# Diagonal key tiles moved from the end of each attention unit to behind its first two full tiles

## The chip, the cores and the metric

The kernel runs on one core of one Trainium2 chip. The metric is the device time of one execution in microseconds (us); the time before is the median of three executions. Five engines of the core matter here: PE (the matrix engine), DVE (the vector engine), ACT (the scalar engine), POOL and SP; the last two mostly issue transfers. Matrix products are written to PSUM, which DVE and ACT then read.

## The reference

A sequence of 2048 tokens of width 256 passes through four residual blocks: attention a, FFN, attention b, FFN. Each block adds its result to x, and each reads a layer-normalised x. Cut to what matters:

```python
# attention (16 heads of 16; a: 4 key/value heads and rotary angles and biases; b: 16 key/value heads)
scores = einsum('bthd,bshd->bhts', q, k) * head_dim ** -0.5
scores = where(tril(ones((S, S))), scores, -inf)      # a query sees itself and earlier keys
out = softmax(scores) @ v ; x = x + out @ Wo.T
# FFN: Wg, Wu, Wd are unpacked from 4-bit codes and scales
x = x + (gelu(xn @ Wg.T) * (xn @ Wu.T)) @ Wd.T
```

The softmax is over all earlier keys, so a query block needs the largest score of each row before its exponentials, and the order in which key tiles are summed is free.

## The kernel before

**Units.** Queries are cut into four blocks b of 512 (`TB`). Sixteen heads are four groups g of four. A *unit* is one (b, g); each attention layer runs its 16 units in order, b outermost. `Attention.run` writes the instruction order of all engines by hand.

**The value pass of a unit** (`value_steps`) goes over key tiles kt of 128 keys: 4b full ones, and four *diagonal* ones, in which the mask cuts a triangle and the queries before the tile are left out: N = 512, 384, 256 and 128 queries. Each key tile takes two *steps* p = 0, 1, each for two of the four heads:

- `pair(kt, p)`: takes a PSUM tile `ps_s`, subtracts the row maxima by a small product (L758, operand `mT`), and adds the scores (L763). For a full tile ACT's exponential (L775, tile `e`) is issued at once. For a diagonal one it is *owed*: four mask products (L645) and the exponential follow when the next `settle()` is called, which is in the next `pair`, in `values`, or ahead of the next maximum if a masked maximum is owed too.
- `values(half)`: sums e times v of the key tile before into the one PSUM tile `ps_av` (L743), 256 queries at a time. Of the third and fourth diagonal tile (256 and 128 queries) all is summed in half 0 and half 1 is empty.

The sums of the last key tile are done by `end()`, with a copy of `ps_av` to `o` on ACT (L790); `divide()` turns `o` (L797) and divides. Both are put into the next unit's steps 0 and 2.

**The maxima of the next unit** (`max_steps`) are computed beside it: for query tile i and key block c the scores again, queries on the partitions (L670), into `ps_s`, and a DVE reduction (L682). For c < b the tile has 512 keys; for c = b, the diagonal, (i + 1) * 128 keys and mask products. The last step, `gather`, joins the partial maxima in five short DVE instructions (L694 to L704) and leaves them in `m_pad`; `turn` transposes `m_pad` on PE (L711, four products), and ACT copies the result to `mT` (L717). The next unit's first `pair` reads `mT`.

**What sets the order.** `ps_s` has three buffers, taken in turn by pairs and maxima: the fourth taker waits until the first one's exponential or reduction is done. `weave(main, side, rest=3)` puts the maxima and other side work (`more`: projections of the next block, the output projection, unpacking of FFN weights) between a step's `pair` and its `values`; three of a unit's maxima go to steps 0 to 2 (four where the next unit is longer by half or a third, six in the step from b = 0 to b = 1), the others are spread over the rest but the last three steps. So the last three steps of a unit have no side work, and `gather` is in the fourth from the end. `turn` stands at the start of the last step, before its `pair`. PE, DVE and ACT each run their instructions in the order written. A unit of block b has 8(b + 1) steps, and as many maxima as its next unit has steps.

**Order of tiles before.** Value pass: full tiles, then the diagonal ones (N = 512, 384, 256, 128). Maxima: full ones, then the diagonal ones with 128, 256, 384 and 512 keys.

Of the kernel before, what the change touches and what calls it, by code (L numbers as in the profile page):

```python
# [31 lines left out]
NT = TB // P  # L32
# [47 lines left out]
def tile_hybrid_layers(  # L80
# [40 lines left out]
    def ps_s():  # L121
        return psum.tile([P, 2, 512], F32, tag="s", name="ps_s", bufs=3)
# [4 lines left out]
    def ps_m():  # L127
        return psum.tile([P, 512], F32, tag="m", name="ps_m")
# [278 lines left out]
    class Attention:  # L407
# [251 lines left out]
        def max_steps(self, b, g):  # L659

            held = {}

            def scores(i, c, p):
                if not held:
                    held["mx"] = self.wk.tile([P, NT, 4, NB], F32, tag="mx", name="mx")
                w = TB if c < b else (i + 1) * P
                self.settle("max")
                pt = ps_s()
                for r in range(2):
                    nc.tensor.matmul(  # L670
                        pt[:, r, :w],
                        lhsT=self.qT[b, g][64 * r : 64 * r + 64, p, i * P : (i + 1) * P],
                        rhs=self.key_rows(c, g, p, r, slice(0, w)),
                        start=True, stop=(c < b),
                    )

                def masked():
                    self.add_mask(pt, 0, w - P)
                    reduced()

                def reduced():
                    nc.vector.tensor_reduce(  # L682
                        held["mx"][:, i, 2 * p : 2 * p + 2, c], pt[:, :, :w], AX.X, ALU.max
                    )

                if c == b:
                    self.owed.append(("max", masked))
                else:
                    reduced()

            def gather():
                self.settle()
                nm = self.wk.tile([P, NT, 4], F32, tag="nm", name="nm")
                nc.vector.tensor_reduce(  # L694
                    nm, held["mx"][:, :, :, : b + 1], AX.X, ALU.max, negate=True
                )

                to = m_pad[:, :, :, :6].rearrange("q t r (p s) -> q t p r s", s=3)
                rest = nm.rearrange("q t (p r) -> q t p r", r=2)
                nc.vector.tensor_copy(to[:, :, :, :, 0], rest)  # L700
                less = self.wk.tile([P, NT, 2, 2], F32, tag="rest", name="rest")
                nc.vector.tensor_tensor(less, rest, to[:, :, :, :, 0], ALU.subtract)
                nc.vector.tensor_copy(to[:, :, :, :, 1], less)
                nc.vector.tensor_tensor(  # L704
                    to[:, :, :, :, 2], less, to[:, :, :, :, 1], ALU.subtract
                )

            def turn():
                pt = ps_m()
                for i in range(NT):  # L710
                    nc.tensor.matmul(  # L711
                        pt[:, i * P : (i + 1) * P],
                        lhsT=m_pad[:, i].rearrange("p r c -> p (r c)"), rhs=ident_b,
                        start=True, stop=True,
                    )
                self.mT[b, g] = self.wk.tile([P, TB], BF16, tag="mT", name="mT")
                nc.scalar.copy(self.mT[b, g], pt)  # L717


            tiles = [(i, c) for c in range(b + 1) for i in range(NT)]  # L720
            steps = [lambda i=i, c=c, p=p: scores(i, c, p) for i, c in tiles for p in range(2)]
            return steps + [gather], turn

        def value_steps(self, b, g):

            nk = NT * (b + 1)
            held = {"pending": []}

            def values(half):

                self.settle()
                kt, q0, es_ = held["pending"][0]
                few = TB - q0 <= TB // 2
                if half == 1:
                    held["pending"].pop(0)
                    if few:
                        return
                elif kt == 0:
                    held["av"] = ps_av()
                own = slice(q0, TB) if few else slice(*((q0, TB // 2), (TB // 2, TB))[half])  # L740
                for j in range(4):
                    h = g if self.first else 4 * g + j
                    nc.tensor.matmul(  # L743
                        held["av"][32 * j : 32 * j + 32, own],
                        lhsT=self.vv[kt // NT][:, kt % NT, h * VW : h * VW + 32],
                        rhs=es_[j // 2][:, j % 2, own],
                        start=(kt == 0 and half == 0), stop=(kt == nk - 1),
                    )

            def pair(kt, p):  # L750
                q0 = max(0, kt - NT * b) * P
                diagonal = kt >= NT * b
                keys = slice((kt % NT) * P, (kt % NT + 1) * P)
                self.settle()
                pt = ps_s()

                for r in range(2):
                    nc.tensor.matmul(  # L758
                        pt[:, r, q0:], lhsT=sel[64 * r : 64 * r + 64, p, :],
                        rhs=self.mT[b, g][64 * r : 64 * r + 64, q0:], start=True, stop=False,  # L760
                    )
                for r in range(2):
                    nc.tensor.matmul(  # L763
                        pt[:, r, q0:], lhsT=self.key_rows(kt // NT, g, p, r, keys),
                        rhs=self.qT[b, g][64 * r : 64 * r + 64, p, q0:],
                        start=False, stop=not diagonal,
                    )
                e = self.wk.tile([P, 2, TB], F32, tag="e", name="e", bufs=4)

                def masked():  # L770
                    self.add_mask(pt, 1, q0)
                    exponentials()

                def exponentials():
                    nc.scalar.activation(e[:, :, q0:], pt[:, :, q0:], AF.Exp, scale=QK_SCALE)  # L775

                if diagonal:
                    self.owed.append(("exp", masked))
                else:
                    exponentials()  # L780
                if p == 0:
                    held["es"] = [e]
                else:
                    held["pending"].append((kt, q0, held["es"] + [e]))

            def end():
                values(0)
                values(1)
                o = pre.tile([P, TB], F32, tag="o", name="o")
                nc.scalar.copy(o, held["av"])  # L790
                held["o"] = o

            def divide():
                o = held["o"]
                pt = ps_m()
                for i in range(NT):
                    nc.tensor.transpose(  # L797
                        pt[:, i * P : (i + 1) * P], o[:, i * P : (i + 1) * P], ident
                    )
                heads = pt.rearrange("p (t j c) -> p t j c", t=NT, c=32)  # L800
                rec = small.tile([P, NT, 4], F32, tag="rec", name="rec")
                nc.vector.reciprocal(rec, heads[:, :, :, HD])
                if g == 0:
                    self.att[b] = pre.tile([P, NT, NG, 4, HD], F32, tag="att", name="att")
                nc.vector.tensor_tensor(
                    self.att[b][:, :, g], heads[:, :, :, :HD],
                    rec.unsqueeze(3).broadcast_to([P, NT, 4, HD]), ALU.mult,
                )

            steps = []  # L810
            for kt in range(nk):
                for p in range(2):
                    scored = lambda kt=kt, p=p: pair(kt, p)
                    steps.append((scored, lambda p=p: values(p)) if kt else scored)
            return steps, end, divide

        def out_steps(self, b):
# [30 lines left out]
        def run(self, extra, beside):  # L848
# [5 lines left out]
            for n, (b, g) in enumerate(units):  # L854
# [3 lines left out]
                if g == 0 and b + 1 < NB:  # L858
                    ahead = self.prep_steps(b + 1)

                    few = -(-(len(ahead) - (7 if self.first else 5)) // 2)
# [7 lines left out]
                maxima, turn = [], None  # L869
                if n + 1 < len(units):  # L870
                    maxima, turn = self.max_steps(*units[n + 1])
                else:
                    more += beside
                steps, end, divide = self.value_steps(b, g)
# [2 lines left out]
                    scored, *summed = steps[at] if isinstance(steps[at], tuple) else (steps[at],)  # L877
                    steps[at] = (scored, step, *summed)
                if turn:
                    scored, summed = steps[-1]  # L880
                    steps[-1] = (turn, scored, summed)
                first = len(maxima) * 3 // len(steps)
                weave(steps[:3], maxima[:first])
                weave(steps[3:], blend(maxima[first:], more) if maxima else more, rest=3)
# [96 lines left out]
    with tc.tile_pool(name="wk1", bufs=2) as wk, tc.tile_pool(name="kv1", bufs=1) as kv:  # L981
        at.wk = at.qpool = wk
        with tc.tile_pool(name="init", bufs=1) as pool:
# [13 lines left out]
            steps, turn = at.max_steps(0, 0)  # L997
# [6 lines left out]
    with tc.tile_pool(name="kv20", bufs=1, reuse_waits="tile") as kv0, tc.tile_pool(  # L1004
# [8 lines left out]
        steps, turn = at.max_steps(0, 0)  # L1013
# [60 lines left out]
```

## Time and profile before

| | us |
|---|---|
| median of 3 executions (lowest to highest) | 1888.08 (1885.3 to 1889.78) |
| the profiled execution, and its span | 1890.76, span 1888.9 |
| PE busy | 1766.7 (94%) |
| DVE busy | 1123.3 (59%) |
| ACT busy | 805.2 (43%) |
| POOL busy | 239.0 (13%) |
| reductions of the maxima, L682 (640) | 658.2 |
| exponentials, L775 (640) | 571.3 |

Stretches of single units, from the first L758 of a unit to that of the next, with the busy time of each engine in it:

| unit (layer, b, g) | stretch, us | length | PE | DVE | ACT |
|---|---|---|---|---|---|
| b, 3, 1 | 1409.45:1455.86 | 46.41 | 45.11 | 36.70 | 30.96 |
| b, 2, 3 (the next one has b = 3) | 1318.48:1358.26 | 39.78 | 36.34 | 35.48 | 22.97 |
| b, 1, 3 (the next one has b = 2) | 1164.22:1193.92 | 29.70 | 25.07 | 26.03 | 14.79 |
| b, 1, 1 | 1104.75:1134.70 | 29.95 | 28.30 | 19.32 | 16.03 |
| b, 0, 2 | 1035.11:1053.13 | 18.02 | 16.72 | 8.60 | 8.05 |

How to read the profile: a group's line gives the kernel line, engine, operation, tiles written and read, count, busy time, mean duration, and the idle time before it with what ended most of it. A wait line gives the waiting instruction, the one waited for, the total, how often, and the longest. A timeline line gives start, duration, engine, line, tiles and count, with the idle time before it in brackets. PE's products are pipelined, so successive ends, not durations, tell how long each took.

### The profile page before, as it was taken

Reading aid. Unit: us, or ns where it says so; the run is one execution under the profiler, and the core shown is the slowest. Engines: PE = TensorE matmul, PEld = TensorE weight load, DVE = VectorE, ACT = ScalarE, POOL = GpSimd, SP = SyncE. Lnnn points to the kernel's source line nnn. Section 1 sums busy time; section 2 is a strip of 40 time slices with the busy share of each in tenths; the row PEclk is TensorE's granted clock in tenths of the full one; section 3 lists DMA queues with packets and bytes.
Section 4 is the critical chain, followed back from the end, with each engine's and each line's share of the span. In section 5 each row is a group of like instructions: output and inputs, shape, how many; then the busy total and the mean of one; then the engine's idle time right before and its main releaser. Section 6 shows DMA issues by size and latency. Waiting matters only on the chain. (4 is left out here: it accounts for less than half of the span.)

```text
span 1888.9 us, 31839 instructions
## 1 busy us (share of the span) xinstructions
PE 1766.7 (94%) x13452; PEld 928.5 (49%) x13452; DVE 1123.3 (59%) x1676; ACT 805.2 (43%) x1069; POOL 239.0 (13%) x437
## 2 busy tenths in 40 slices
PE   5788889999999999999998898999999999999999
PEld 3344444444444456656564444444444444756656
DVE  4567687778786253544445667766877715363442
ACT  1334455555667531222213355556566662131221
POOL 4111321210001011112101010010000001011110
PEclk8889999999999999999998999999999999999999
DMA  4421310310101100001303232041000010000000
GB/s 100 108 60 37 68 52 23 63 35 24 35 24 35 45 6 1 1 0 42 81 1 74 62 72 54 12 90 33 15 13 2 2 46 1 11 1 11 7 6 12
DMA packets 42271, 64.24 MB, mean 34 GB/s; under 512 B 13840, under 2 KB 20880, under 8 KB 41872
## 3 DMA queue, kind: packets, MB, share of 16 engines
q1 hardware_dynamic: 33488, 45.93, 8.2%
q0 software_dynamic: 7680, 15.74, 5.0%
q8 instruction: 106, 1.74, 0.4%
q10 hardware_dynamic: 960, 0.52, 0.1%
q14 instruction: 37, 0.30, 0.1%
HBM read 44.24 MB, written 17.83 MB: 33 GB/s over the span
## 5 line engine op out<-in xcount | busy, mean ns | idle before, releaser
L682 DVE TENSOR_REDUCE mx<-ps_s 128x2 f32<-128x1024 f32 (+3 forms) x640 | 658.2, 1060 | 221.0 <-PE ps_s L645 116.0
L775 ACT ACTIVATE e<-ps_s 128x1024 f32<-128x1024 f32 (+3 forms) x640 | 571.3, 897 | 422.6 <-PE ps_s L763 244.8
L743 PE MATMUL ps_av<-e,v 128*32 128x256 f32 (+1 forms) x4608 | 365.2, 384 | 3.4 <-ACT e L775 3.4
L763 PE MATMUL ps_s<-qT,kT 64*128 64x512 f32 (+3 forms) x1280 | 341.7, 527 | 0.0
L670 PE MATMUL ps_s<-kT,qT 64*128 64x512 f32 (+3 forms) x1280 | 269.2, 423 | 52.3 <-DVE mx L682 22.8
L758 PE MATMUL ps_s<-mT,sel 64*128 64x512 bf16 (+3 forms) x1280 | 232.7, 358 | 27.3 <-ACT mT L717 10.1
L934 PE MATMUL ps_s<-xnT,wg 128*128 128x512 f32 x512 | 242.1, 595 | 0.0
L934 PE MATMUL ps_s<-xnT,wu 128*128 128x512 f32 x512 | 240.6, 592 | 0.0
L670 PEld LDWEIGHTS ps_s<-kT,qT 64*128 64x128 f32 x1280 | 130.1, 188 | 161.6 <-ACT e L775 66.5
L758 PEld LDWEIGHTS <-sel 64*128 64x128 bf16 x1280 | 75.0, 93 | 251.2 <-issue 242.3
L942 DVE TENSOR_TENSOR t<-ps_s,t 128x512 f32<-128x512 f32 x128 | 88.1, 688 | 164.5 <-POOL t L941 162.7
L940 ACT ACTIVATE t<-ps_s 128x512 f32<-128x512 f32 x128 | 76.2, 595 | 251.8 <-PE ps_s L934 251.3
L943 ACT ACTIVATE t<-t 128x512 f32<-128x512 f32 x128 | 80.6, 629 | 200.7 <-DVE t L942 200.7
L934 PEld LDWEIGHTS ps_s<-xnT,wu 128*128 128x128 f32 x512 | 97.3, 190 | 122.7 <-issue 122.7
L941 POOL TENSOR_SCALAR t<-t 128x512 f32<-128x512 f32 x128 | 79.1, 618 | 573.0 <-ACT t L940 572.5
L743 PEld LDWEIGHTS ps_av<-e,v 128*32 128x32 f32 x4608 | 95.0, 108 | 109.1 <-issue 89.5
L934 PEld LDWEIGHTS ps_s<-xnT,wg 128*128 128x128 f32 x512 | 96.0, 192 | 106.0 <-issue 104.0
L944 DVE SCALAR_TENSOR_TENSOR t<-t,ps_s 128x512 f32<-128x512 f32 x128 | 88.0, 688 | 89.0 <-ACT t L943 89.0
L763 PEld LDWEIGHTS ps_s<-qT,kT 64*128 64x128 f32 x1280 | 130.5, 199 | 0.0
L959 PE MATMUL ps_m<-wd,inter 128*128 128x256 f32 x512 | 114.5, 380 | 0.0
L959 PE MATMUL ps_av<-wd,inter 128*128 128x256 f32 x512 | 114.5, 380 | 0.0
L959 PEld LDWEIGHTS ps_av<-wd,inter 128*128 128x128 f32 x512 | 96.7, 190 | 17.1 <-issue 4.5
(125 smaller groups left out, 1179.9 us busy)
## 6 DMA issues: line engine op xcount, KB each, us to landing
qT<-h SPq DMA_DIRECT2D x256, 64.0 KB, 2.2
kT<-h POOLq DMA_DIRECT2D x96, 128.0 KB, 5.9
h<-high SPq DMA_DIRECT2D x24, 256.0 KB, 2.6
h<-low SPq DMA_DIRECT2D x24, 256.0 KB, 2.5
wd<-wd_kept SPq DMA_DIRECT2D x2, 2048.0 KB, 7.8
wd_kept<-dq_d SPq DMA_DIRECT2D x4, 512.0 KB, 2.7
out<-x SPq DMA_DIRECT2D x16, 128.0 KB, 1.7
x<-x SPq DMA_DIRECT2D x3, 512.0 KB, 5.4
```

The costliest lines, as they stand in the source:

```text
L670: nc.tensor.matmul(pt[:, r, :w], lhsT=self.qT[b, g][64 * r : 64 * r + 64, p, i * P : (i + 1) * P], rhs=self.key_rows(c, g, p, r, slice(0, w)),
L682: nc.vector.tensor_reduce(held["mx"][:, i, 2 * p : 2 * p + 2, c], pt[:, :, :w], AX.X, ALU.max)
L743: nc.tensor.matmul(held["av"][32 * j : 32 * j + 32, own], lhsT=self.vv[kt // NT][:, kt % NT, h * VW : h * VW + 32], rhs=es_[j // 2][:, j % ...
L758: nc.tensor.matmul(pt[:, r, q0:], lhsT=sel[64 * r : 64 * r + 64, p, :], rhs=self.mT[b, g][64 * r : 64 * r + 64, q0:], start=True, stop=False,)
L763: nc.tensor.matmul(pt[:, r, q0:], lhsT=self.key_rows(kt // NT, g, p, r, keys), rhs=self.qT[b, g][64 * r : 64 * r + 64, p, q0:], start=Fals ...
L775: nc.scalar.activation(e[:, :, q0:], pt[:, :, q0:], AF.Exp, scale=QK_SCALE)
L934: nc.tensor.matmul(pt[:, k, :], lhsT=w[:, c, fc * P : (fc + 1) * P], rhs=self.xnT[b][:, c, :], start=(c == 0), stop=(c == 1),)
L941: nc.gpsimd.tensor_scalar(t, t, GELU_A, 1.0, ALU.mult, ALU.add)
L942: nc.vector.tensor_tensor(t, gate, t, ALU.mult)
L943: nc.scalar.activation(t, t, AF.Tanh, scale=GELU_C)
L944: nc.vector.scalar_tensor_tensor(t, t, 1.0, gate, ALU.add, ALU.mult)
L959: nc.tensor.matmul(po[:, :D], lhsT=inter[:, fc, i * P : (i + 1) * P], rhs=wd[:, fc, :], start=(fc == 0), stop=(fc == NFC - 1),)
```

## The change

In a unit with full tiles the value pass now takes the first two full key tiles, then the four diagonal ones, then the other full ones. The maxima take the first two full tiles, then the diagonal ones in falling size (512, 384, 256, 128 keys), then the other full ones. For b = 0 there are no full tiles: the value pass is as before, and the maxima run in reverse. The start and stop marks of the accumulation follow the first and last tile of the new order. `turn` moves from the start of the last step to the middle of the last but one: behind its `pair`, ahead of its `values`. The number and kind of instructions is the same.

```diff
-            tiles = [(i, c) for c in range(b + 1) for i in range(NT)]
+            full = [(i, c) for c in range(b) for i in range(NT)]
+            tiles = full[:2] + [(i, b) for i in reversed(range(NT))] + full[2:]
...
-            nk = NT * (b + 1)
+            full = [*range(NT * b)]
+            order = full[:2] + [*range(NT * b, NT * (b + 1))] + full[2:]
...
-                elif kt == 0:
+                elif kt == order[0]:
                     held["av"] = ps_av()
...
-                        start=(kt == 0 and half == 0), stop=(kt == nk - 1),
+                        start=(kt == order[0] and half == 0),
+                        stop=(kt == order[-1] and (few or half == 1)),
...
-            for kt in range(nk):
+            for kt in order:
                 for p in range(2):
                     scored = lambda kt=kt, p=p: pair(kt, p)
-                    steps.append((scored, lambda p=p: values(p)) if kt else scored)
+                    first = kt == order[0]
+                    steps.append(scored if first else (scored, lambda p=p: values(p)))
...
                 if turn:
-                    scored, summed = steps[-1]
-                    steps[-1] = (turn, scored, summed)
+                    scored, summed = steps[-2]
+                    steps[-2] = (scored, turn, summed)
```

## The prediction

> **What bounds the kernel now.** First the page: PE is busy for 1766.7 of 1888.9 us, and the largest group elsewhere is DVE's reductions.
>
> ```profile
> span 1888.9 us, 31839 instructions
> PE 1766.7 (94%) x13452; PEld 928.5 (49%) x13452; DVE 1123.3 (59%) x1676; ACT 805.2 (43%) x1069; POOL 239.0 (13%) x437
> L682 DVE TENSOR_REDUCE mx<-ps_s 128x2 f32<-128x1024 f32 (+3 forms) x640 | 658.2, 1060 | 221.0 <-PE ps_s L645 116.0
> ```
>
> The waits say what PE's attention work waits for: PSUM tiles held by ACT or DVE, and `mT` and `m_pad` between units.
>
> ```profile
> PEld ps_s L670 <- ACT e L775: 66.5, 176, 1.6
> PEld ps_s L670 <- DVE mx L682: 60.0, 128, 1.6
> PE ps_s L758 <- ACT mT L717: 10.1, 29, 0.7
> PE ps_m L711 <- DVE m_pad L704: 8.3, 7, 3.5
> ```
>
> Then the timeline: a plain full step, the middle of the diagonal ones, and the seam between two units (all from layer b, b = 3).
>
> ```profile
> 1422.05 0.40 PE L743 MATMUL ps_av<-e,v 128*32 128x256 f32 x4
> 1422.42 0.58 PE L763 MATMUL ps_s<-qT,kT 64*128 64x512 f32 x2
> 1422.83 0.48 PE L670 MATMUL ps_s<-kT,qT 64*128 64x512 f32 x2
> 1423.24 0.64 PE L743 MATMUL ps_av<-e,v 128*32 128x256 f32 x8
> ...
> 1448.72 0.29 PE L645 MATMUL ps_s<-mask_t,mask_w 64*128 64x64 bf16 x8
> 1449.05 1.02 ACT L775 ACTIVATE e<-ps_s 128x1024 f32<-128x1024 f32 x1 [0.67 <-PE ps_s L645]
> 1449.55 0.47 PE L763 MATMUL ps_s<-qT,kT 64*128 64x384 f32 x2
> 1450.13 0.50 PE L670 MATMUL ps_s<-kT,qT 64*128 64x512 f32 x2
> ...
> 1454.55 0.23 DVE L704 TENSOR_TENSOR m_pad<-rest,m_pad 128x16 bf16<-128x16 f32 x1
> 1455.46 0.40 PE L711 MATMUL ps_m<-ident_b,m_pad 128*128 128x128 bf16 x4
> 1455.90 0.58 ACT L717 CAST mT<-ps_m 128x512 bf16<-128x512 f32 x1 [0.45 <-PE ps_m L711]
> 1456.54 0.39 PE L758 MATMUL ps_s<-mT,sel 64*128 64x512 bf16 x2 [0.32 <-ACT mT L717]
> 1457.45 0.43 PE L743 MATMUL ps_av<-e,v 128*32 128x128 f32 x8
> 1459.73 0.51 PE L670 MATMUL ps_s<-kT,qT 64*128 64x512 f32 x2 [0.27 <-ACT e L775]
> ```
>
> I count PE by differences of ends. The sums end at 1422.45, the pair at 1423.00, the maximum at 1423.31, the next sums at 1423.88: pair 0.55, maximum 0.31 (0.24 where no buffer was awaited), sums 0.57, a step 1.36 to 1.44. In the same way a pair with N = 384, 256, 128 takes 0.44, 0.34, 0.28, sums of 128 queries 0.36, masks 0.07 each. In a queue the reductions take 1.14 each, as the chain shows where DVE binds (the unit b, 1, 3):
>
> ```profile
> 1170.75 12.54 DVE mx L682 x11
> ```
>
> At 1.15 maxima a step that is 1.31 us of DVE, just below PE's step. So PE leads by little, and a lighter PE step makes DVE or ACT the bound.
>
> **The change part by part.** No instruction is added or removed; no DMA moves, so SP and POOL keep their order. All cost is in waits. I write a "full-seam unit" for one whose predecessor has b of 1 or more (22 of 32).
>
> *Seam, gain 0.64.* Before, the first pair of a unit ends 0.95 after its predecessor rather than 0.55 (the 0.32 wait for `mT`). Then ACT holds the buffers: the second maximum takes 0.46 for 0.24, the third 0.85 for 0.24 (at 1459.73 it waits for an exponential queued behind the copy `o`); with 0.05 at the first, 1.28. After the change `turn` (0.33) is followed by sums 0.57, a pair 0.55 and sums 0.57, 1.69 us, while ACT needs about 1.02 for the exponential ahead and 0.58 for `mT`, begun with `turn`: the 0.40 goes. `end` has two full sums, 1.14 for 0.36, which hides all but the third maximum's wait: the exponential before it starts behind `o` and ends some 1.1 after its pair, PE is there after 0.24 + 0.55, 0.64 stays. 1.28 - 0.64 = 0.64.
>
> *Diagonal steps, loss 0.86.* The rule read at 1450.13: masks end at 1449.01, the exponential runs 1449.05 to 1450.07, and the next but one maximum, which needs its buffer, ends 0.61 after its pair rather than 0.25: a wait of 0.36. Before, such terms in the unit b, 3, 1 are 0.27 (a pair behind two small maxima), 0.10, 0.22, 0.36, 0.15: 1.10. After, both passes shrink together and the maxima wait behind exponentials of 1.02, 1.02, 0.81, 0.81 and 0.60 us with pairs of 0.55, 0.44, 0.44, 0.34 and 0.34 for cover: 0.20, 0.32, 0.10, 0.21, 0.23, then 0.06. The half-1 steps without sums, which before lay in the tail without maxima, now lie among full maxima: over four steps PE has about 4.0 us (1.28, 0.66, 1.24, 0.85), DVE 4 x 1.23 less overlaps; PE waits 0.14 + 0.07 + 0.14 for reductions and 0.22 + 0.27 for full exponentials, 0.84. Sum 1.96, less 1.10. The trace has no diagonal pair beside a shrinking diagonal maximum: the bounds are 0 (side work covers as before) and 1.7 (nothing overlaps). I take 0.86, from the neighbouring rows' own durations.
>
> *Turn behind the pair of the last step but one.* Waiting there, it holds sums, the last step and the next unit's first pair. From the last maximum to `turn` PE has, for b of 2 and 3, sums 0.57, pair 0.55, sums 0.57, pair 0.55, sums 0.57, pair 0.55 = 3.36; DVE needs 0.1 + 1.23 + 1.2 for the five gather instructions = 2.55. No wait. For b = 1 two of the sums are empty and one short, 2.0 at the end against 2.55, or 3.7 with two maxima queued: 0.5 to 1.6, less what projections (1.9 each) cover. I take 0.5 against 0.15 before: loss 0.35.
>
> By the Trainium skill (TensorE: Matmul & The Clock Gate, Part 3, The mechanism) matmuls are strict FIFO, "no reordering", though weight loads may pass; the timeline agrees, for nothing of PE passes a waiting L711. Could PE go round it, the 0.35 above and the turn's share of the next class would be zero and the forecast about 4 us lower.
>
> *Units by class.* Block 3 and 2, not g = 3 (12): 0.86 - 0.64 = +0.22 each, +2.6. Block 1, not g = 3 (6): +0.22 + 0.35, +3.4; two of them follow b = 0 and gain only 0.40 at the seam, +0.5. Block 1 into 2 (2): DVE binds; its chain (work 25.9 in a queue, idle 1.0 at the start, 1.7 to 1.85 within) ends as late as before, and behind it come `turn`, sums, pair, sums = 2.1 rather than 1.1: +1.15 each, +2.3. Block 2 into 3 (2): same tail, but diagonal maxima no longer end a stretch that DVE binds: +0.2 each, +0.4. Block 0 into 1 (2): DVE's chain as long, tail +0.25: +0.5. Last unit of each layer: 0.40 and 0.29 (divide behind `o`) gone, 0.4 for the last full exponential: -0.3 each, -0.6. Block 0 (6): the reverse order lets the small reductions end last, so turn waits of 1.68, 0.79 and 0.24 and buffer waits of some 5 us near the end shrink, while full maxima in the first steps cost about 0.95 each: -2.8, the least certain. The first maxima of layer a, alone on PE: the first reduction starts later, +0.3. FFN stages: nothing moves.
>
> Sum: 2.6 + 3.4 + 0.5 + 2.3 + 0.4 + 0.5 - 0.6 - 2.8 + 0.3 = +6.6 us. The profiled execution's 1890.76 (span 1888.9 and 1.86 around it) becomes 1897.4. It lies 2.7 above the median of the runs; on the median 1888.08 the forecast is 1894.7, 0.35% slower. About 0.2% (3.8 us) is what a measurement of this kernel can tell from no change.
>
> The skill also says (Perfetto Trace Analysis, Optimization Strategy) that stages with different bounds may gain by interleaving. That speaks for moving small maxima among the full ones, and the classes with b rising agree only in part: what DVE regains in the middle it loses in a longer tail. If interleaving won there, the 2.3 + 0.4 would be about -2 and the sum 2.
>
> **Rivals.** *Faster, by the seam.* The place: diagonal steps whose waits stay at 1.10 because projections and unpacking stand between. Then 18 units gain 0.86 each, 15.5, and the block-1 turns do not wait, 2.1: 6.6 - 17.6 = -11, 1877. For it: blocks 0 to 2 have much side work. Against: blocks 3 have little, and most of what there is runs on DVE. It decides where a unit's diagonal waits stay below about 1.96 - 6.6 / 18 = 1.6.
>
> *No change.* Turn waits in block 1 covered by projections and DVE stretches no worse: 6.6 - 2.1 - 2.3 = +2.2, 1890.3. For it: one of three block-1 units in layer b waits at `turn` now. Against: the two sums that covered are gone.
>
> *Much slower, DVE becomes the bound.* A reduction is 1.14 in a queue at 1.15 to 1.22 a step, so a backlog after the light steps melts by under 0.1 a step; at 0.8 or more of it `turn` waits in blocks 2 and 3 too, some 0.6 in 12 units, +7.2: 1902. For it: unpacking puts more on DVE in layer a (38.6 against 36.7 us a unit). Against: three buffers let PE run only that far ahead.
>
> **How the numbers follow.** Main case 0.44, much slower 0.18, no change 0.22, faster 0.16. Slower by over 0.2%: 0.44 + 0.18 = 0.62; within: 0.22; faster: 0.16. The range leaves out half the faster case and the far end of the slower: 1883 to 1905. The cases from the main one's own bounds reach 1890 to 1901.
>
> **What would show it.** Right: no wait of L758 for `mT` in units after b = 1 or more; more waits of L670 and L758 for L775 and L682 in steps 5 to 14 of a unit; L711 waiting for `m_pad` in block-1 units for 0.5 us; unit b, 3, 1 near 46.6, unit b, 1, 3 near 30.8. Wrong: b = 3 units shorter than 46.2, or reductions queued without a gap in them.

## The result and the profile after

Five executions of the changed kernel have a median of 1899.58 us (1897.06 to 1900.07), five of the kernel before 1889.78 (1885.3 to 1890.63): a ratio of 1.0054, 95% interval 1.0039 to 1.0068. The profiled execution took 1900.07 us, 9.3 more than that of before. The forecast was +0.35%, in a range that holds the time. But the total hides errors that cancelled: where I expected most of the loss there was none, and the seams between blocks cost far more, in part for a reason that the forecast doesn't have.

The page of the changed kernel: span, engines and the reductions. (From L720 on, line numbers are 1 to 5 higher than before: L758, L763, L743, L775 are now L762, L767, L746, L779.)

```profile
span 1898.3 us, 31835 instructions
PE 1774.0 (93%) x13452; PEld 921.8 (49%) x13452; DVE 1119.1 (59%) x1676; ACT 808.2 (43%) x1069; POOL 238.8 (13%) x437
L682 DVE TENSOR_REDUCE mx<-ps_s 128x2 f32<-128x1024 f32 (+3 forms) x640 | 657.2, 1061 | 234.7 <-PE ps_s L670 124.7
```

The same 13452 products keep PE busy 7.3 us longer, and its idle time grew by only 2.1: most of the loss is products whose records are longer. Of the waits, the one of L758 (now L762) for `mT` fell from 10.1 us (29 times) to 1.3 (the first units of the two layers), and the one of the maxima for DVE grew from 22.8 to 27.7. The first line is the trace before, the others the trace after:

```profile
PE ps_s L670 <- DVE mx L682: 22.8, 47, 1.2
```

```profile
PEld ps_s L670 <- ACT e L779: 74.5, 177, 1.2
PEld ps_s L670 <- DVE mx L682: 58.4, 109, 1.6
PE ps_s L670 <- DVE mx L682: 27.7, 57, 1.2
PE ps_m L711 <- DVE m_pad L704: 8.3, 8, 2.0
PE ps_s L762 <- ACT mT L717: 1.3, 2, 0.7
```

**Where it went.** Unit lengths of the two traces, from the first L758 (L762) of a unit to that of the next, summed by the classes of the prediction (the stretches ahead of the prediction start and end up to 0.7 us before that product; their lengths are the same):

| class (units) | forecast, us | trace after less trace before, us |
|---|---|---|
| blocks 2 and 3, not g = 3 (12) | +2.6 | -1.9 |
| block 1, not g = 3 (6) | +3.9 | +0.8 |
| block 1 into 2 (2) | +2.3 | +3.4 |
| block 2 into 3 (2) | +0.4 | +2.8 |
| block 0 into 1 (2) | +0.5 | +5.1 |
| block 0 (6) | -2.8 | +2.9 |
| last unit of each layer, and FFN | -0.6 | -2.6 |
| start, to the first unit | +0.3 | -1.0 |
| sum | +6.6 | +9.4 |

**The granted clock.** The trace after shows PE's clock at half speed for 92.9 us in all, the trace before for 69.5 (one execution each), mostly at the start of a layer and in its block 0. Stretches of two units follow; columns are start and end, length, busy time (and instructions) of PE, weight loads, DVE, ACT, POOL, granted clock, DMA share, GB/s. First b, 0, 3 and b, 3, 1 before:

```profile
1053.45:1073.19 19.74, 14.42 (x184) 8.27 (x184) 16.96 (x23) 6.60 (x11) 0.00 (x0) 1.00 0.10 28
1410.13:1456.54 46.41, 45.11 (x505) 20.39 (x505) 36.70 (x39) 30.96 (x35) 0.00 (x0) 1.00 0.05 13
```

and after:

```profile
1058.00:1081.19 23.19, 20.22 (x191) 10.97 (x191) 16.98 (x23) 6.67 (x10) 0.00 (x0) 0.63 0.09 24
1421.35:1467.50 46.15, 45.16 (x508) 19.69 (x505) 36.69 (x39) 31.10 (x35) 0.00 (x0) 1.00 0.05 13
```

The first is 3.45 us longer with a clock of 0.63; the second, at full clock, is 0.26 shorter. In the timeline of b, 0, 3 after, sums of 256 queries take 1.08 us and not 0.64; the first line is PE's longest gap in the unit before the clock fell, near 1063.3:

```profile
1060.20 0.39 PE L762 MATMUL ps_s<-mT,sel 64*128 64x512 bf16 x2 [0.56 <-DVE mx L682]
...
1071.53 1.08 PE L746 MATMUL ps_av<-e,v 128*32 128x256 f32 x8
1074.90 0.80 PE L670 MATMUL ps_s<-kT,qT 64*128 64x512 f32 x2 [0.89 <-DVE mx L682]
1076.03 0.80 PE L670 MATMUL ps_s<-kT,qT 64*128 64x512 f32 x2 [0.34 <-DVE mx L682]
```

So I set two theories against each other. *Waits*: the loss is what the prediction names, engines waiting in another order. *Clock*: PE is used more thinly where DVE binds, its granted clock falls, and the products behind take longer.

### The profile page after: what moved, and what is told of

It reads as the page before. It is cut to its first block, busy times and chain, and to the rows that moved or that the text cites. A ratio compares the mean times of both kernels' runs of the same rounds, so it can differ in the third digit from the quotient of the medians.

```text
span 1898.3 us, 31835 instructions
## 1 busy us (share of the span) xinstructions
PE 1774.0 (93%) x13452; PEld 921.8 (49%) x13452; DVE 1119.1 (59%) x1676; ACT 808.2 (43%) x1069; POOL 238.8 (13%) x437
## 5 line engine op out<-in xcount | busy, mean ns | idle before, releaser
L779 ACT ACTIVATE e<-ps_s 128x1024 f32<-128x1024 f32 (+3 forms) x640 | 569.9, 896 | 425.4 <-PE ps_s L645 263.2
L746 PE MATMUL ps_av<-e,v 128*32 128x256 f32 (+1 forms) x4608 | 364.0, 386 | 2.9 <-ACT e L779 2.9
L767 PE MATMUL ps_s<-qT,kT 64*128 64x512 f32 (+3 forms) x1280 | 342.4, 530 | 0.0
L670 PE MATMUL ps_s<-kT,qT 64*128 64x512 f32 (+3 forms) x1280 | 275.7, 434 | 60.8 <-DVE mx L682 27.7
L762 PE MATMUL ps_s<-mT,sel 64*128 64x512 bf16 (+3 forms) x1280 | 233.6, 360 | 21.5 <-DVE mx L682 8.8
L762 PEld LDWEIGHTS <-sel 64*128 64x128 bf16 x1280 | 72.5, 93 | 253.8 <-issue 248.8
L746 PEld LDWEIGHTS ps_av<-e,v 128*32 128x32 f32 x4608 | 98.2, 109 | 114.6 <-issue 86.7
L767 PEld LDWEIGHTS ps_s<-qT,kT 64*128 64x128 f32 x1280 | 131.2, 200 | 0.0
```

The costliest lines, as they stand in the source:

```text
L670: nc.tensor.matmul(pt[:, r, :w], lhsT=self.qT[b, g][64 * r : 64 * r + 64, p, i * P : (i + 1) * P], rhs=self.key_rows(c, g, p, r, slice(0, w)),
L746: nc.tensor.matmul(held["av"][32 * j : 32 * j + 32, own], lhsT=self.vv[kt // NT][:, kt % NT, h * VW : h * VW + 32], rhs=es_[j // 2][:, j % ...
L762: nc.tensor.matmul(pt[:, r, q0:], lhsT=sel[64 * r : 64 * r + 64, p, :], rhs=self.mT[b, g][64 * r : 64 * r + 64, q0:], start=True, stop=False,)
L767: nc.tensor.matmul(pt[:, r, q0:], lhsT=self.key_rows(kt // NT, g, p, r, keys), rhs=self.qT[b, g][64 * r : 64 * r + 64, p, q0:], start=Fals ...
```

## The experiments

Each kernel was timed beside the kernel before on the same chip. The diffs are against the changed kernel unless the text says otherwise. The conditions name the unit (b, g), for the maxima the unit that they belong to.

**1. Where does it sit?** The change in neighbouring units of the same block alone, and its complement:

```diff
+            tiles = full + [(i, b) for i in range(NT)]
+            if b > 0 and g > 0:                          # complement: b == 0 or g == 0
                 tiles = full[:2] + [(i, b) for i in reversed(range(NT))] + full[2:]
...
+            order = full + [*range(NT * b, NT * (b + 1))]
+            if b > 0 and g < 3:                          # complement: b == 0 or g == 3
                 order = full[:2] + [*range(NT * b, NT * (b + 1))] + full[2:]
...
-                if turn:
+                if turn and (b > 0 and g < 3):           # complement: b == 0 or g == 3
                     scored, summed = steps[-2]
                     steps[-2] = (scored, turn, summed)
+                elif turn:
+                    scored, summed = steps[-1]
+                    steps[-1] = (turn, scored, summed)
```

> The change alone where two neighbouring units have the same block b of 1 or more (18 of 31 seams); the orders of before elsewhere. By the trace after, those units together moved by about -0.6 (block 3), -1.3 (block 2) and +1.3 us (block 1), so the kernel should stand within 3 us of before (1886 to 1892). Waits theory as predicted (+0.22 a unit in blocks 2 and 3, +0.57 in block 1): +6 us, 1895. Clock theory: the granted clock stays as before, 0.982.

> The change alone in the other units: block 0, and the seams at which b rises (13 of 31). If the loss sits there, as the unit lengths of the trace after say (+5.3 for 0 into 1, +3.4 for 1 into 2, +2.8 for 2 into 3, +2.2 within block 0), nearly the whole +9 us comes with it: 1897 to 1901, with a mean granted clock near 0.976. If the loss is spread over all units as predicted, +0 to +2 us.

Measured: 1887.85 us, ratio 1.0000 (0.9987 to 1.0014), against 1901.96, ratio 1.0081 (1.0063 to 1.0099). The loss sits in block 0 and where b rises. In same-block units the change is worth nothing that this run shows; the +6.5 forecast for them was wrong. The complement's mean, 1901.8 us, lies 2.9 above that of the whole change, at a mean clock of 0.976 against 0.978; the run of the same-block part has no gain that would account for it.

The complement in two parts: block 0 with the seam into block 1 (maxima new for b == 0 and (1, 0), turn for b == 0), and the seams 1 into 2 and 2 into 3 (value pass and turn new for b > 0 and g == 3, maxima for b > 1 and g == 0):

> The change alone in block 0 and at the seam from block 0 into 1 (reversed maxima, the turn one sum earlier). Clock theory: this is where the granted clock is lost, the mean falls to about 0.978 and the kernel stands 5 to 8 us above before, 1892 to 1895. Waits theory as predicted (-2.8 + 0.5 + 0.3): -2 us, 1885.

> The change alone at the seams from block 1 into 2 and 2 into 3 (4 of 31). Waits theory: the longer tail behind DVE's chain, +1.15 at 1 into 2 and +0.2 to +0.9 at 2 into 3 in each layer, +3 to +5 us, 1890 to 1892, at an unchanged granted clock. Clock theory: the thin stretches there cost granted clock as well, mean 0.981 or less and +7 us or more.

Measured: 1893.2, ratio 1.0036 (1.0022 to 1.0049), and 1896.2, ratio 1.0051 (1.0036 to 1.0066). Together 0.87%, about the complement's 0.81%: the parts add up. For the block-0 part the waits forecast had the wrong sign.

**2. The parts by kind.** The turn alone (the before-orders of tiles), the maxima alone, values and turn without the maxima, and the changed kernel with the turn in its old place:

```diff
# turn alone: the first two hunks; maxima alone: the second and the third; values and turn: the first
-            tiles = full[:2] + [(i, b) for i in reversed(range(NT))] + full[2:]
+            tiles = full + [(i, b) for i in range(NT)]
...
-            order = full[:2] + [*range(NT * b, NT * (b + 1))] + full[2:]
+            order = full + [*range(NT * b, NT * (b + 1))]
...
# turn in its old place
-                    scored, summed = steps[-2]
-                    steps[-2] = (scored, turn, summed)
+                    scored, summed = steps[-1]
+                    steps[-1] = (turn, scored, summed)
```

> The tile orders of before; only the turn of the maxima moves, from the start of the last step to the middle of the last but one. Waits theory: the 0.40 us that each of some 22 unit starts spends on mT goes, for the turn now has sums of 0.57 and a short pair of 0.35 behind it; in block 0 and at rising seams the turn waits as long as before, +0.2 each: -6 to -8 us, 1881 to 1884. Rival: the maxima are not ready 0.57 us earlier, PE waits at the turn instead, and the time stays within 2 us of before.

> Only the maxima take the new order (diagonal ones behind two full ones, falling in size); the value pass and the turn stay as before. Waits theory: the units keep their light value steps at the end, so no longer tail at rising seams; the small maxima no longer fill the light steps, full ones do, and DVE binds there: +0.2 to +0.5 a unit in blocks 2 and 3, 0 to +1 in block 0; 1889 to 1895 at an unchanged granted clock of 0.983. Clock theory: if the reversed maxima of block 0 thin PE out, the mean granted clock falls below 0.981 and each 0.001 of it costs 1.2 us more.

> The new order of the value pass and the new place of the turn, with the maxima in the order of before. If the maxima of the old order, small ones last, and the light value steps early suit each other (full maxima beside light values bind on DVE early, small maxima leave it idle late): worse than the changed kernel, 1900 or more. If the reversed maxima of block 0 are what costs granted clock: mean clock 0.981 or more and 1893 to 1897.

> The changed kernel with the turn back at the start of the last step. Waits theory: in blocks 1 to 3 the last step is now full (pair 0.55 and sums 0.57 behind the turn, mT needs 0.7), so no unit waits for mT and block 1 waits 0.5 less for the maxima; in block 0 the 0.3 for mT returns but the turn waits less: within 3 us of the changed kernel, 1896 to 1900. If the place of the turn itself is the gain of the change, 5 to 8 us slower than the changed kernel.

| kernel | median, us | ratio to before (95%) |
|---|---|---|
| turn alone | 1886.25 | 0.9999 (0.9986 to 1.0011) |
| maxima alone | 1901.99 | 1.0083 (1.0067 to 1.0100) |
| values and turn | 1911.29 | 1.0124 (1.0108 to 1.0139) |
| changed, turn in its old place | 1899.81 | 1.0062 (1.0048 to 1.0075) |
| changed | 1899.58 | 1.0054 (1.0039 to 1.0068) |

The two orders need each other: values and turn without the maxima is clearly worse than the whole change, and the maxima alone is worse in the mean (1902.2 against 1898.9 us), though the intervals of the two ratios touch. The value order without the moved turn was not run. With the small value steps early and the small maxima still last, PE waits more for DVE, at the turn and at the pairs (first fence, the waits of the run with values and turn; the same two lines are 8.3 and 7.1 us in the trace before, 8.3 and 8.8 in the trace after). In b, 3, 1 the unit is 1.03 longer than before (second, the stretch). Reductions without a gap are no sign of this by themselves: before, six, seven and six follow each other in that unit as well (here nine at most).

```profile
PE ps_m L711 <- DVE m_pad L704: 18.7, 14, 3.5
PE ps_s L762 <- DVE mx L682: 18.5, 46, 0.6
```

```profile
1425.37:1472.81 47.44, 45.62 (x508) 20.45 (x505) 36.63 (x39) 31.11 (x35) 0.00 (x0) 1.00 0.05 13
```

The turn's place is worth nothing that these runs show in the new order (1.0062 against 1.0054): there the full last step hides `mT` wherever the turn stands (with the turn in its old place PE waits 3.3 us for it, 8 times, never behind a unit of blocks 1 to 3). In the old order it is worth some 0.4 us in most units of blocks 2 and 3: b, 3, 1 takes 46.01 for 46.41. But the time as a whole didn't move: in the profiled execution the units of block 0 and 1 gave it back, and b, 0, 3 grew from 19.74 to 22.24 at a granted clock of 0.74.

**3. The clock by itself.** Idle bf16 products keep PE busy in the two units from block 0 into 1: first into the maxima's own tile, then into a spare one ahead of it, where PE waits for a buffer.

```diff
# first form; the second writes a spare ps_m tile before settle("max"), for maxima 1 to 5 and 9 on
                 self.settle("max")
                 pt = ps_s()
+                if (b, g) == (1, 0):
+                    for _ in range(2):
+                        nc.tensor.matmul(pt[:, 0, :], lhsT=ident_b,
+                            rhs=mask_w.rearrange("p k a c -> p (k a c)"), start=True, stop=True)
```

> The changed kernel with two idle bf16 products of 512 columns put ahead of each maximum of block 1, group 0, in both layers (they write the tile that the maximum then overwrites): some 0.43 us more PE work for each of 32 maxima, 14 us in two units. Clock theory: in the unit b, 0, 3 of the changed kernel PE is so thinly used that its granted clock falls to half for 17 us; the filler keeps it up, the granted clock of that unit rises from 0.63 to 0.9 or more and the unit falls from 23.2 us to 20 or 21 although it has more work. Waits theory: the unit is bound by DVE's reductions whatever PE's clock; it stays at 23 us or grows by a few us, and a kernel time of 1900 to 1906.

> The changed kernel with idle bf16 products into a spare tile put ahead of 12 of the 16 maxima of block 1, group 0, where PE waits for a buffer anyway (24 products of 0.21 us, 5.2 us in each of two units). Clock theory: the granted clock of the unit b, 0, 3 returns from 0.63 to 0.9 or more and its length from 23.2 to 20 to 21.5 us, that of a, 0, 3 from 22.6 to about 21; the kernel gains 3 to 5 us on the changed kernel, to 1894 to 1896. Waits theory: DVE binds these units, the fillers hide in PE's waits and nothing changes, 1898 to 1900.

Measured: 1906.1 us, ratio 1.0103 (1.0078 to 1.0127), and 1900.92, ratio 1.0077 (1.0060 to 1.0094). Of the clock theory the granted clock came true, 0.99 to 1.00 in these units in both forms, at a mean of 0.984 over the executions, but not the shorter unit; the times lie at or just above the upper end of what the waits theory said. The unit b, 0, 3 in the first form, then a, 0, 3 and b, 0, 3 in the second:

```profile
1059.56:1085.29 25.73, 23.10 (x220) 10.00 (x223) 17.58 (x23) 6.62 (x10) 0.00 (x0) 1.00 0.08 22
```

```profile
121.40:144.40 23.00, 20.38 (x211) 9.12 (x213) 17.05 (x23) 6.59 (x10) 0.00 (x0) 1.00 0.09 24
1058.46:1081.46 23.00, 20.38 (x212) 9.13 (x215) 17.05 (x23) 6.61 (x10) 0.00 (x0) 1.00 0.10 25
```

The fillers are not free, so this can't decide. What decides is that the two units of block 0 into 1, with the same work, occur in several kernels at several clocks, and in both orders. The new order, in the block-0 run and in the complement run of experiment 1:

```profile
118.42:139.35 20.93, 15.73 (x191) 8.65 (x190) 16.77 (x23) 6.59 (x10) 0.00 (x0) 0.90 0.10 27
1055.88:1076.81 20.93, 15.57 (x190) 8.96 (x190) 16.86 (x23) 6.60 (x10) 0.00 (x0) 0.92 0.09 27
```

```profile
117.93:141.09 23.16, 20.18 (x191) 11.08 (x191) 16.96 (x23) 6.60 (x10) 0.00 (x0) 0.63 0.10 27
1058.60:1079.56 20.96, 15.79 (x190) 8.63 (x190) 16.77 (x23) 6.60 (x10) 0.00 (x0) 0.90 0.10 27
```

The order of before, in the run with fillers at the later seams below, which leaves these units as they were:

```profile
119.03:139.54 20.51, 15.72 (x184) 8.87 (x184) 16.96 (x23) 6.59 (x11) 0.00 (x0) 0.92 0.11 27
1058.23:1081.47 23.24, 20.16 (x184) 11.11 (x184) 17.06 (x23) 6.59 (x11) 0.00 (x0) 0.63 0.09 25
```

| granted clock of the unit (0, 3) | order of before, layer: us | order of the change, layer: us |
|---|---|---|
| 1.00 | b: 19.73, 19.74, 19.74 | b: 19.84 (turn in its old place) |
| 0.90 to 0.92 | a: 20.51 | a: 20.93; b: 20.93, 20.96 |
| 0.84 | a: 20.77, 20.77; b: 21.73 | |
| 0.70 to 0.74 | a: 22.64, 22.68 | a: 22.39 |
| 0.63 | b: 23.24 | a: 23.16; b: 23.19 |

At one clock the two orders differ by -0.1 to +0.4 us, less than cases of the old order at 0.84 differ among themselves (1.0), while the clock moves the old order by 3.5 us, and the new one by 2.3 between 0.90 and 0.63. The 3.45 us of b, 0, 3 need nothing but the clock: at 0.63 the old order is as long. And since the old order falls to 0.63 there too, this fall can't be laid to the change: ten such units of the old order have 0.63 to 1.00, mean 0.85, six of the change 0.63 to 0.92, mean 0.79. At full clock PE is busy for 73% of the unit in the old order and 72% in the new one with the old turn.

The seams that rise later, with fillers in the stretch that DVE binds:

```diff
# against the run with the change at these seams alone
+                n = held["n"] = held.get("n", -1) + 1
+                if b > 1 and g == 0 and 11 < n < 8 * b + 4:
+                    if n == 12:
+                        held["idle"] = ps_m()
+                    for _ in range(4 - b):
+                        nc.tensor.matmul(held["idle"], lhsT=ident_b,
+                            rhs=mask_w.rearrange("p k a c -> p (k a c)"), start=True, stop=True)
```

> The run with the change at the seams from block 1 into 2 and 2 into 3 alone (1896.2, clock 0.980), with idle bf16 products into a spare tile ahead of the maxima in the stretch that DVE binds (two of 0.21 us ahead of 8 maxima, one ahead of 16, about 3.4 us in each of four units). Clock theory: the half-clock windows near 274 and 435 us of layer a go, the unit a, 2, 0 falls from 46.5 to about 44 and the kernel by 2 to 4 us to 1892 to 1894, clock 0.982 or more. Waits theory: the fillers hide or add work, 1896 to 1899.

Measured: 1906.96 us, ratio 1.0098 (1.0084 to 1.0112). In the profiled execution the half-clock windows near 274 and 435 us went, and a, 1, 3 and a, 2, 0 ran at full clock. The two units without fillers, then with them:

```profile
243.08:276.38 33.30, 25.59 (x288) 12.64 (x287) 28.26 (x39) 14.82 (x19) 4.43 (x9) 0.97 0.13 33
276.38:320.90 44.52, 40.80 (x432) 20.20 (x429) 33.68 (x54) 24.39 (x30) 6.69 (x12) 0.99 0.09 25
```

```profile
244.31:278.63 34.32, 29.24 (x304) 13.38 (x304) 28.54 (x39) 14.38 (x19) 4.43 (x9) 1.00 0.12 30
278.63:322.56 43.93, 40.20 (x432) 19.93 (x429) 33.70 (x54) 24.82 (x30) 6.69 (x12) 1.00 0.11 27
```

The unit a, 2, 0 fell by 0.6 us, not by 2.5: the 46.5 of the expectation counts the last pair of a, 1, 3 into it. The fillers stand in a, 1, 3, which grew by 1.0. In layer b, where the clock was full anyway, 3.4 us of fillers made b, 1, 3 3.1 us longer (30.37 to 33.43) and b, 2, 3 4.0 (40.57 to 44.54). The total rose, and the mean clock of the executions did not (0.980 in both). A wait of PE is not room for other PE work when the work stands in order ahead of the product that DVE needs next.

**4. The clock over all executions.** Each execution has a mean granted clock. Over the 42 executions of the kernel before, 0.980 to 0.986, a clock lower by 0.001 goes with a time higher by 1.0 us; over all kernels, within each, by 0.96. With that slope the means stand as follows (an estimate: it takes the slope to hold between kernels):

| kernel | mean time, us | mean clock | brought to 0.983 |
|---|---|---|---|
| before (42) | 1887.5 | 0.9834 | 1887.9 |
| changed (5) | 1898.9 | 0.9778 | 1893.9 |
| same-block part (10) | 1887.1 | 0.9827 | 1886.8 |
| block-0 part (5) | 1893.2 | 0.9808 | 1891.1 |
| later seams (4) | 1896.1 | 0.9798 | 1893.0 |
| turn alone (10) | 1886.7 | 0.9810 | 1884.8 |

Of the changed kernel's 11.4 us above these executions of before, some 5.4 go with the clock and 6.0 are left. The means of before on the three chips differ by 2.0 us (1886.4 to 1888.4), so the split is good to some 2 us.

**5. What is worth keeping.** From the kernel before, the turn moved where the next unit has the same block (b > 0 and g < 3) and nowhere else, so that block 0 and its clock are left alone:

```diff
# against the kernel before
-                if turn:
+                if turn and (b > 0 and g < 3):
+                    scored, summed = steps[-2]
+                    steps[-2] = (scored, turn, summed)
+                elif turn:
                     scored, summed = steps[-1]
                     steps[-1] = (turn, scored, summed)
```

> The tile orders of before; the turn moves ahead of the sums of the last step but one only where the next unit has the same block b of 1 or more (18 seams). Waits theory: the trace of the run that moved every turn shows -0.4 us in each such unit of blocks 2 and 3 and -0.2 a unit in block 1 of layer b, -6 us in all; without the turns of block 0 and of the rising seams the granted clock stays at 0.983 or 0.984: 1880 to 1883, 0.2 to 0.4% faster than before. Rival: the gain is given back in side work or granted clock, within 0.1% of before.

Measured: 1885.28 us against 1888.09, ratio 0.998 (0.9969 to 0.9990): faster than both kernels, by 0.2% against the kernel before: the near end of the forecast, and 2.3 us above the times that it named. In layer b the units of blocks 2 and 3 whose turn moved are 0.38 to 0.43 shorter each, those of block 1 change by -0.41, +0.17 and -0.41. In the same units the whole change was worth nothing (experiment 1), so there the old order of tiles with the moved turn looks the better one, though the two intervals touch. The seam of b, 3, 1 in it: the turn has masks, sums of 0.64 and a short pair behind it, and the first L762 of the next unit waits for nothing.

```profile
1450.65 0.40 PE L711 MATMUL ps_m<-ident_b,m_pad 128*128 128x128 bf16 x4
1451.14 0.64 PE L746 MATMUL ps_av<-e,v 128*32 128x256 f32 x8
...
1451.97 0.38 PE L762 MATMUL ps_s<-mT,sel 64*128 64x512 bf16 x2
```

## Why the prediction was right, and where it was not

**Seam, gain 0.64: right.** In the trace after, the turn is followed by full sums, a pair and sums, and the next unit starts without a wait:

```profile
1465.48 0.40 PE L711 MATMUL ps_m<-ident_b,m_pad 128*128 128x128 bf16 x4
1465.81 0.64 PE L746 MATMUL ps_av<-e,v 128*32 128x256 f32 x8
...
1466.93 0.64 PE L746 MATMUL ps_av<-e,v 128*32 128x256 f32 x8
1467.50 0.39 PE L762 MATMUL ps_s<-mT,sel 64*128 64x512 bf16 x2
```

The 0.40 went. From the first to the fifth pair b, 3, 1 now takes 6.96 us (1421.35 to 1428.31) for 6.58, with 0.64 more of sums in it (two tiles' halves 1.00 for 0.36): 0.26 gained, 0.66 in all. But the cause was put in the wrong part: it is the longer tail that hides `mT`, not the turn's place, as the run with the old place shows.

**Diagonal steps, loss 0.86: the sum that failed.** The waits after are near what I worked out, 2.14 in all for 1.96. Read as before, from the excess of each maximum or pair over its free cost, they are 0.24, 0.33, 0.14, 0.25, 0.27 where exponentials hold the buffers (forecast 0.20, 0.32, 0.10, 0.21, 0.23), and 0.91 in the steps without sums and behind them (forecast 0.84). Two of them, at 1432.12 (the maximum ends 0.55 after its pair, not 0.22) and 1442.44 (0.62, not 0.24):

```profile
1431.55 0.47 PE L767 MATMUL ps_s<-qT,kT 64*128 64x384 f32 x2
1432.12 0.44 PE L670 MATMUL ps_s<-kT,qT 64*128 64x384 f32 x2
...
1441.72 0.60 PE L767 MATMUL ps_s<-qT,kT 64*128 64x512 f32 x2
1442.44 0.49 PE L670 MATMUL ps_s<-kT,qT 64*128 64x512 f32 x2
```

What I sized wrong is the old order's side. The unit moved by -0.26, so with a gain of 0.66 at the seam the rest lost 0.40, not 0.86, and not the 1.04 that waits of 2.14 after and 1.10 before would give. The 1.10 leaves out the first maximum of 128 keys, which also waits behind a full exponential: it ends 0.32 after its pair, where the next such maximum takes 0.06; and 0.08 more at the first maximum of 256. From the trace before:

```profile
1441.67 0.58 PE L763 MATMUL ps_s<-qT,kT 64*128 64x512 f32 x2
1442.09 0.48 PE L670 MATMUL ps_s<-kT,qT 64*128 64x128 f32 x2
...
1443.19 0.58 PE L763 MATMUL ps_s<-qT,kT 64*128 64x512 f32 x2
1443.61 0.22 PE L670 MATMUL ps_s<-kT,qT 64*128 64x128 f32 x2
```

With the 0.13 that the sixth pair of the unit waits before (behind a step with two full maxima) and not after, that is 0.47; the last 0.2 I can't place. The class as a whole is not this unit twelve times. The six units of block 3 moved by -0.6 together, +0.2 each being forecast; in block 2, a, 2, 0 and b, 2, 0 grew by 1.1 and 1.0, and a, 2, 1 and a, 2, 2 fell by 0.9 and 2.5 at full clock. No run shows why a, 2, 2 gains so much; every run with the whole change in same-block units has it, at 40.8 us for 43.3. A unit of block 3 below 46.2 was one of my signs of being wrong: b, 3, 1 is one, with 46.15.

**Turn in block 1, 0.5 against 0.15: right in size.** The turn waits 0.92, 0.56, 0.47 in layer a and 1.08 in one unit of layer b, 3.0 over six units, against 0.46 before. What the units lost, 0.8 in all, can't be set against it: the clock of three of them changed (a, 1, 1 from 0.96 to 1.00, and 2.1 us shorter; a, 1, 2 from 1.00 to 0.95, and 2.6 longer; b, 1, 0 from 0.95 to 1.00).

**Seam from block 1 into 2, +1.15: right where the clock held.** b, 1, 3 went from 29.70 to 30.86, with `m_pad` last and 2.02 us from the turn to the next unit (forecast 2.1):

```profile
1201.77 0.40 PE L711 MATMUL ps_m<-ident_b,m_pad 128*128 128x128 bf16 x4 [1.06 <-DVE m_pad L704]
...
1203.79 0.39 PE L762 MATMUL ps_s<-mT,sel 64*128 64x512 bf16 x2
```

In layer a, at a clock of 0.97, the same seam cost 2.2.

**Seam from block 2 into 3, +0.2: too small.** At full clock b, 2, 3 lost 0.9. I gave it a regained middle that the trace does not show.

**Seam from block 0 into 1, +0.25: too small, for want of the clock.** The two traces differ by 1.6 and 3.45 us, and their granted clock went from 0.84 to 0.74 and from 1.00 to 0.63. At 0.63 the old order takes 23.24 and the new 23.19; what the waits add at one clock is too small to be read from these units, so the 0.25 itself stays open.

**Block 0, -2.8: failed, in sign.** The turn waits shrank as said (1.68, 0.79 and 0.24 before; after, 0.64 and 0.09 for the last two, none for the first, and 0.58 in another unit). But b, 0, 2 is 0.67 longer at a full clock, and so it is, by 0.67 to 0.68, in every run with the whole change in block 0: there the waits that the order adds outweigh those that it takes. That it is the full maxima in the first steps, which I had set at 0.95 each, is likely, but no run takes it apart.

**The clock was not in the forecast.** I wrote that all cost is in waits. Among 69.5 us of half clock in the trace before, I took what was there as given. That fillers in thin stretches bring the clock back is shown (0.99 to 1.00 in four units of four); that a lower clock makes the same unit longer is shown, by 19.7 to 23.2 us in the old order alone. That the changed kernel has the lower clock is shown in the mean of its executions, 0.9778 against 0.9834; how much of the total goes with it, some 5 us, rests on the slope over executions, and which units lose it is open. The Trainium skill (TensorE: Matmul & The Clock Gate, A second HAM failure mode) describes a clock that oscillates when PE idles for short moments between groups of products. The trace agrees: in b, 0, 3 after, the clock fell without any gap of PE above 0.6 us before it in the unit.

The forecast of the total stood by luck: the same-block classes were 7.6 us too dear, block 0 and the rising seams 13.8 too cheap, and the start and the last units with the FFN 3.3 too dear (the FFN stages had 6.8 us less of half clock than in the trace before).

## What to carry to other kernels

Where two streams share buffers, try a small step in one beside a small step in the other: here the small value steps among full maxima cost twice as much as both orders together (1.24% against 0.54%, the turn moved in both). Read the granted clock beside a unit's length before explaining the length by waits: one unit here takes 19.7 to 23.2 us with its clock, without any change to it. When a change has several parts, price them apart: here a single moved turn in 18 places was worth 0.2%, and the whole change cost nearly three times that.

## What I had not expected

The half-clock windows come in steps of 3.4 us, and whether one falls in a given unit differs between executions: the executions of the kernel before spread from 1883.7 to 1893.5 us, and their mean clock follows the time at 1.0 us per 0.001. Idle products in PE's waits cost about their own length where the clock was full already (3.1 and 4.0 us for 3.4), and no run with them was faster than the same kernel without.
